# A planned order of work, by due time instead of merge order, and three small matmul groups of a head made one

## The chip, the cores and the metric

The kernel runs on one core of one Trainium2 chip. The metric is the device time of one execution in microseconds (us); the median of three runs of the kernel before is 2750.61 us (2749.08 to 2750.61). One execution was taken with the hardware profiler. Engines are named as the profile names them: PE (TensorE, matrix products), PEld (its weight loads), DVE (VectorE), ACT (ScalarE), POOL (GpSimd) and SP (SyncE, which here only issues DMA transfers). SBUF is the on-chip working memory, PSUM the eight banks into which PE writes its products. 0.2%, 5.5 us, is about what a measurement of this kernel can tell from no change.

## The reference

Four transformer layers in a row work on x of shape 4 x 512 x 512 with a context of 4 x 64 x 512, all in float32.

- Layer 0: twice a cross attention to the context (16 heads of width 128, with one learned extra key and value per head), each behind a layer norm, then a GELU MLP of width 2048.
- Layer 1: a small cross attention of width 512 without heads, added with a factor alpha.
- Layer 2: x is the latent; its queries attend to the context (under an integer mask) and to x itself, 16 heads of width 32; then an RMS norm and an MLP of width 2048.
- Layer 3: a cross attention to the context under a boolean mask, 16 heads of width 32, and an MLP of width 2048, both behind layer norms.

```python
# layer 0, one of its two cross attentions (cut)
qh = (q_in @ wq + bq).reshape(b, q_len, H, K)
kh = jnp.concatenate([(kv_in @ wk + bk).reshape(b, t, H, K), bias_k], axis=1)
vh = jnp.concatenate([(kv_in @ wv + bv).reshape(b, t, H, K), bias_v], axis=1)
weights = jax.nn.softmax(jnp.einsum('bqhk,bthk->bhqt', qh, kh) / scale, axis=-1)
return jnp.einsum('bhqt,bthk->bqhk', weights, vh).reshape(b, q_len, H * K) @ wo + bo
```

## The kernel before

The kernel is a recording and a planner. The layer functions do not issue instructions; each `with pe(us)`, `with dve(n)`, `with either(n)` and so on records one operation (`Op`) with the engines on which it may run, a duration for planning, and the buffers that it takes and reads. An operation on PE can hold several matmuls; these are issued together, and this text calls them a group. `Plan.merge` then lays the recorded operations of streams that may run beside each other (`pl.beside`, for example the keys, the values and the token norms of layer 0) into one list. How far each stream stands at which share of the others is set by the table `PACES`: thirteen regions, two or three streams each, seventeen numbers per stream. An operation's `pos` is its place in that list, in microseconds of PE work.

`Plan.attempt` walks through time with a heap per engine. When an engine is free it takes the first ready operation of its heap that finds room in PSUM and SBUF and does not run more than `AHEAD` us (loads `AHEAD_LOAD`) of `pos` ahead of the oldest unfinished one. The heaps are in the order of the merged list (`op.n`, line 417). An operation that may run on two engines goes to whichever takes it first; the sums in SBUF (`added`, line 1046, recorded at line 1048) run on DVE or POOL, copies out of PSUM (`move`, lines 575 and 576) on ACT or DVE. A bank of PSUM or a block of SBUF is given back in the moment in which its last reader ends (line 519), while an operation that reads a result becomes ready 0.06 us after its maker ended (0.2 us after PE), plus 0.1 us if it goes to PE. What `attempt` puts out is the order in which each engine gets its instructions; on the chip every engine works through its own queue in order, and waits where a semaphore says so.

Layer 0 does not multiply x with wq. For each head it takes the head's keys K (built at line 717 as the product of wk and the context), multiplies them with the transposed wq of that head (line 812: four matmuls of 130 columns in two groups, each with a PSUM bank of its own) and with bq (line 823: one matmul, a third group and bank). For the values it takes V of a head (line 717 again, with wv) and multiplies it with that head's rows of wo (line 877). Two heads share a bank, one in its lower and one in its upper 64 partitions; there is one group for each of the two batches of a pair. Line 891 multiplies the extra value with wo. The attention itself (lines 933, 1038, 1367 and the softmax between them) and the MLPs (line 1089) use Strassen-like products of seven instead of eight parts, and the sums at line 1048 make their operands and put their results together. In layer 2, line 1571 makes the scores of four heads in four banks, line 1582 takes their maxima, line 1594 the exponentials, and line 1628 transposes these.

Three small transfers are issued ahead of the plan: alpha by ACT's queue, and the masks mk_i and mk_b by POOL's queue. All others are operations of SP in the plan.

Of the kernel before, what the change touches and what calls it, by code (L numbers as in the profile page):

```python
# [209 lines left out]
class Op:  # L210
    __slots__ = ("n", "pos", "engines", "calls", "wait", "next", "takes", "uses", "table", "ready", "start", "on", "load", "port")


class Plan:
# [11 lines left out]
    def __init__(self, sbuf, ahead, ahead_load, reserve, full, patience, near, paces):  # L226
        self.reserve, self.full = reserve, full * BLOCK
        self.sbuf = Memory(BLOCK, sbuf)
        self.psum = Memory(1024, 4)
        self.ahead, self.ahead_load = ahead, ahead_load  # L230
        self.patience, self.near, self.paces = patience, near, paces
        self.ops, self.regions = [], []
        self.pos = 0.0
# [143 lines left out]

    def order(self):
# [21 lines left out]
    def attempt(self, narrow):  # L400
# [3 lines left out]
        dma_free = 0.0  # L404
# [7 lines left out]
        out = []  # L412
        busy = dict.fromkeys(heaps, 0.0)

        def arm(op):
            for e in op.engines:
                heapq.heappush(heaps[e], (op.n, op))
# [6 lines left out]
        while left:  # L424
            progress = True
            while progress:
# [8 lines left out]
                for e, heap in heaps.items():  # L435
# [5 lines left out]
                    while heap and len(skipped) < 60:  # L441
                        n, op = heapq.heappop(heap)
                        if begun[n]:
                            continue
                        skipped.append((n, op))
                        if op.ready > now + 1e-9:
                            continue
                        if op.pos > limit + (ahead_load if op.load else ahead):
                            break
# [19 lines left out]
                    if second is not None and (choice is None or choice.pos > second.pos + 6.0):  # L469
                        choice = second  # L470
                    for n, op in skipped:
                        if op is not choice:
                            heapq.heappush(heap, (n, op))
# [35 lines left out]
            while events and events[0][0] <= now + 1e-9:  # L509
                _, kind, n = heapq.heappop(events)  # L510
                if kind != 1:
# [4 lines left out]
                for b in op.uses:  # L516
                    b.left -= 1
                    if b.left == 0:
                        b.mem.give(b)
# [128 lines left out]
def stack(nc, const, sbuf, psum, a, out):  # L648
# [15 lines left out]
    alpha = const.tile([P, 1], FP, name="alpha")  # L664
    nc.scalar.dma_start(out=alpha, in_=a["alpha"].to_broadcast([P, 1]))

    mk_i = const.tile([P, B * T], I32, name="mk_i")
    nc.gpsimd.dma_start(out=mk_i, in_=a["mask_i"].to_broadcast([P, B * T]))
    mk_b = const.tile([P, B * T], U8, name="mk_b")
    nc.gpsimd.dma_start(out=mk_b, in_=a["mask_b"].to_broadcast([P, B * T]))  # L670
    pl = Plan(BLOCKS, AHEAD, AHEAD_LOAD, RESERVE, FULL, PATIENCE, NEAR, PACES)
    sb, ps = pl.sb, pl.ps
    ctxT = pl.held(const.tile([P, NC * B * T], FP, name="ctxT")).v(NC, B * T)
    mterm2, mterm3 = (pl.held(const.tile([P, B * T], FP, name=f"mterm{i}")).v(B, T) for i in (2, 3))

# [110 lines left out]
    def l0_keys(n, half, bp):  # L786
# [6 lines left out]
        for j in range(4):  # L793
            for e in range(2):
# [12 lines left out]
                made = []  # L807
                for r in range(2):
                    p = ps()
                    with pe(4 * SHORT) as o:  # L810
                        for c in range(2):
                            o.matmul(
                                p[:, c * KP : (c + 1) * KP],
                                wq[:, (2 * r + c) * P : (2 * r + c + 1) * P],
                                kT.v(),
                                start=True,
                                stop=True,
                            )
                    made.append(p[:, : 2 * KP].split(2, KP))

                p = ps()
                with pe(2 * SHORT) as o:
                    o.matmul(
                        p[:, :KP], col(f"L0_xattn_bq{n}", h).to_broadcast([P, P]), kT.v(), start=True, stop=True
                    )

# [26 lines left out]
    def l0_values(n, half, bp):  # L853
# [6 lines left out]
        for j in range(HH):  # L860
# [11 lines left out]
            if j % 2:  # L872
                for i in range(2):
                    p = ps()
                    with pe(PAIR + 0.04) as o:
                        for e in range(2):
                            o.matmul(
                                p[e * T : (e + 1) * T, :],
# [4 lines left out]
                            )  # L883
                    with either(D) as o:
                        o.move(U[i].v(HH // 2, D)[:, j // 2, :].k(j // 2), p.v())
# [601 lines left out]
    def l2_context():  # L1487
# [5 lines left out]
        with pool(256) as o:  # L1493
            o.tensor_tensor(apart[:, 256:].k(1), row[:, 256:], row[:, :256], ALU.subtract)
        with dve(256) as o:
            o.tensor_scalar(mterm2, mk_i.rearrange("p (b s) -> p b s", b=B), 0.0, -3.0e38, ALU.is_equal, ALU.mult)
# [192 lines left out]
    def l3_context():  # L1689
        row = load_row("L3_xattn_v_b")  # L1690
        with dve(256) as o:
            o.tensor_scalar(mterm3, mk_b.rearrange("p (b s) -> p b s", b=B), 0.0, LOWEST, ALU.is_equal, ALU.mult)
# [127 lines left out]
    def a0():  # L1820
        l1.append(l1_project())
        l2_context()
# [6 lines left out]
    def a3(pair):  # L1829
# [21 lines left out]
AHEAD, AHEAD_LOAD, RESERVE = 170.0, 90.0, 2  # L1851
FULL = 24


PATIENCE, NEAR = 7.0, 37.0
# [3 lines left out]
        [2, 7, 11, 22, 33, 23, 51, 60, 57, 66, 72, 60, 77, 83, 93, 101, 104],  # L1859
        [-4, 6, 18, 24, 27, 26, 37, 42, 48, 66, 62, 76, 74, 81, 86, 92, 97],  # L1860
        [-1, 1, 14, 14, 28, 38, 37, 50, 54, 53, 61, 74, 76, 83, 90, 96, 111],
    ],
    [
        [-1, 8, 26, 23, 26, 28, 35, 43, 60, 61, 72, 61, 72, 72, 77, 79, 88],
        [18, 28, 34, 25, 39, 34, 60, 34, 55, 62, 73, 70, 77, 98, 92, 102, 111],
    ],
    [
        [4, 13, 16, 19, 27, 36, 40, 46, 37, 58, 68, 63, 67, 76, 86, 86, 87],
# [103 lines left out]
```

## Time and profile before

| | us |
|---|---|
| median of three runs | 2750.61 |
| the profiled execution | 2748.76 |
| its span, first to last instruction | 2747.0 |
| PE busy | 2701.2 (98%) |
| DVE busy | 2044.7 (74%) |
| POOL busy | 1323.0 (48%) |
| ACT busy | 931.5 (34%) |
| SP's queue (q1): share of 16 DMA engines | 19.4% |

In the profile's rows, a line such as L1089 is a line of the kernel file, `out<-in` are the tensors written and read (`arena` is all of the planned SBUF, `banks` all of PSUM), `xN` a number of hardware records. A float32 matmul leaves two records, since the hardware makes it in two passes; a transpose leaves one. The idle time of an engine stands behind the second bar with what ended it. Matmuls are pipelined, so that the busy time of PE also covers short waits between them.

### The profile page before, as it was taken

What the parts mean: (1) busy time and instruction counts of PE and PEld (TensorE: products, weight loads), DVE (VectorE), ACT (ScalarE), POOL (GpSimd) and SP (SyncE); (2) the same over time, 40 slices, a digit from 0 to 9 for tenths busy, and PEclk for the clock granted to TensorE, in tenths of its full rate; (3) what the DMA queues carried; (4) which work ended last, traced back from release to release, by engine and by line L of the source; (5) the groups of instructions that cost most, each with busy time, mean ns of one, the idle gap of its engine ahead of it and who ended that gap; (6) DMA issues with size and microseconds to landing.
All of it is one profiled execution on the core that took longest, in us unless ns stands there. A gap on an engine that the chain in (4) does not pass through costs nothing. (4 is left out here: it accounts for less than half of the span.)

```text
span 2747.0 us, 34916 instructions
## 1 busy us (share of the span) xinstructions
PE 2701.2 (98%) x12012; PEld 1648.4 (60%) x12012; DVE 2044.7 (74%) x3661; ACT 931.5 (34%) x1759; POOL 1323.0 (48%) x1465
## 2 busy tenths in 40 slices
PE   8999999999999999999999999999999999999999
PEld 6877778788854455556555665555544545454444
DVE  6788778786864577776787678687877878878655
ACT  3223242142331114453463255154523223333211
POOL 5567576574842262333335232424745485646421
PEclk9999999999999999999999999999999999999999
DMA  7222423243121020010102011110211120202200
GB/s 242 84 89 81 131 77 115 64 134 93 50 62 57 16 69 20 20 59 14 44 25 88 8 31 45 56 32 24 70 50 35 41 67 20 58 8 84 77 16 31
DMA packets 230368, 164.06 MB, mean 60 GB/s; under 512 B 9088, under 2 KB 198656, under 8 KB 230192
## 3 DMA queue, kind: packets, MB, share of 16 engines
q1 hardware_dynamic: 229824, 161.52, 19.4%
q8 instruction: 96, 1.57, 0.2%
q14 instruction: 80, 0.66, 0.1%
q0 software_dynamic: 80, 0.16, 0.0%
q10 hardware_dynamic: 288, 0.15, 0.0%
HBM read 157.60 MB, written 4.19 MB: 59 GB/s over the span
## 5 line engine op out<-in xcount | busy, mean ns | idle before, releaser
L1048 POOL TENSOR_TENSOR arena<-arena 128x256 f32<-128x256 f32 (+4 forms) x1016 | 1064.1, 1064 | 970.5 <-DVE arena L576 169.8
L1089 PE MATMUL banks<-arena 128*128 128x512 f32 x2688 | 1201.9, 594 | 7.9 <-DVE arena L1108 2.6
L1089 PEld LDWEIGHTS banks<-arena 128*128 128x128 f32 x2688 | 497.8, 190 | 578.3 <-issue 497.6
L1048 DVE TENSOR_TENSOR arena<-arena 128x256 f32<-128x256 f32 (+4 forms) x664 | 574.1, 879 | 89.9 <-POOL arena L1048 24.8
L575 ACT COPY arena<-banks 128x512 f32<-128x512 f32 (+4 forms) x563 | 280.5, 516 | 793.9 <-PE banks L1089 196.3
L1367 PE MATMUL banks<-arena 128*128 128x256 f32 x1792 | 408.3, 380 | 3.2 <-DVE arena L938 1.5
L1367 PEld LDWEIGHTS banks<-arena 128*128 128x128 f32 x1792 | 336.2, 190 | 79.8 <-issue 21.9
L576 DVE COPY arena<-banks 128x512 f32<-128x512 f32 (+2 forms) x353 | 213.1, 613 | 160.2 <-PE banks L1089 52.5
L1124 ACT ACTIVATE arena<-arena,cols 128x512 f32<-128x512 f32 x192 | 138.0, 722 | 313.2 <-DVE arena L1048 172.9
L1108 DVE TENSOR_TENSOR arena<-banks,arena 128x512 f32<-128x512 f32 x240 | 163.8, 685 | 90.6 <-PE banks L1089 76.2
L933 PE MATMUL banks<-arena 128*128 128x260 f32 x896 | 212.0, 385 | 0.3 <-DVE arena L938 0.2
L1594 ACT ACTIVATE arena<-banks,arena 128x512 f32<-128x512 f32 x256 | 174.7, 687 | 95.1 <-DVE arena L1584 49.5
L933 PEld LDWEIGHTS banks<-arena 128*128 128x128 f32 x896 | 163.5, 188 | 36.0 <-ACT arena L575 3.0
L1582 DVE TENSOR_REDUCE arena<-banks 128x1 f32<-128x512 f32 x256 | 167.5, 681 | 13.3 <-PE banks L1571 12.2
L717 PE MATMUL banks<-ctxT,arena 128*128 128x128 f32 (+1 forms) x1152 | 164.1, 292 | 12.1 <-DMA arena<-in_L_wv 6.5
L717 PEld LDWEIGHTS banks<-ctxT,arena 128*128 128x128 f32 x1152 | 148.8, 194 | 29.5 <-issue 11.2
L1628 PEld LDWEIGHTS banks<-ident,arena 128*128 128x128 f32 x1024 | 116.5, 141 | 81.6 <-issue 35.1
L1628 PE MATMUL banks<-ident,arena 128*128 128x128 f32 x1024 | 140.9, 276 | 3.5 <-ACT arena L1594 2.9
L717 PE MATMUL banks<-arena 128*128 128x512 f32 (+2 forms) x432 | 140.4, 482 | 0.0
L1147 DVE TENSOR_TENSOR arena<-banks,arena 128x512 f32<-128x512 f32 x144 | 98.2, 685 | 50.2 <-PE banks L1089 50.1
L1605 POOL TENSOR_TENSOR arena<-arena 128x256 f32<-128x256 f32 x64 | 39.5, 617 | 188.6 <-DVE arena L1584 160.2
L717 PEld LDWEIGHTS banks<-arena 128*128 128x128 f32 x432 | 72.4, 191 | 68.3 <-issue 65.7
(155 smaller groups left out, 2528.4 us busy)
## 6 DMA issues: line engine op xcount, KB each, us to landing
arena<-in_L_w SPq DMA_DIRECT2D x192, 256.0 KB, 3.3
arena<-in_L_wk SPq DMA_DIRECT2D x80, 256.0 KB, 4.9
arena<-in_L_wv SPq DMA_DIRECT2D x64, 256.0 KB, 5.6
arena<-in_L_wqT SPq DMA_DIRECT2D x64, 256.0 KB, 5.5
arena<-in_L_wo SPq DMA_DIRECT2D x64, 256.0 KB, 5.7
arena<-in_L_wq SPq DMA_DIRECT2D x32, 256.0 KB, 3.3
arena<-in_L_wo SPq DMA_DIRECT2D x8, 1024.0 KB, 5.4
arena<-in_L_wv SPq DMA_DIRECT2D x6, 1024.0 KB, 5.7
```

Of the source, the lines that this page charges most:

```text
L575: "ACT": lambda e, out, in_: e.copy(out, in_),
L576: "DVE": lambda e, out, in_: e.tensor_copy(out, in_),
L717: o.matmul(dst, lhs(c), rhs(c), start=(c == 0), stop=(c == NC - 1))
L933: o.matmul(p[:, : 2 * KP], lhs(c), rhs(c, b % 2), start=(c == 0), stop=(c == 1))
L1048: o.tensor_tensor(out, x, y, op)
L1089: o.matmul(p.v(), lhs(c), rhs(c), start=(c == 0), stop=(c == 1))
L1108: o.tensor_tensor(t.v(), p.v(), y.v(), ALU.add)
L1124: o.activation(g[f].v(), src.v(), func, bias=col(b1, q * NC + f))
L1367: o.matmul(p[:, i * 256 : (i + 1) * 256], lhs(c), rhs(c), start=(c == 0), stop=(c == 1))
L1582: o.tensor_reduce(m[:, i : i + 1].k(i), banks[i].v(), AX.X, ALU.max)
L1594: o.activation(y.v(), banks[i].v(), AF.Exp, bias=nm[:, i : i + 1].k(i), scale=qs, accum_out=sums[:, i : i + 1].k(i),)
L1628: o.transpose(p[:, c * P : (c + 1) * P], e[i][:, c * P : (c + 1) * P], ident)
```

## The change

Five things are edited. The planner's heaps for work that touches neither PSUM nor PE are now sorted by due time: the earliest `pos` at which PE needs the result, less the durations on the way. Memory is given back later: 0.06 us after its last reader ended (0.2 us after PE), and 0.1 us more for a PSUM bank. An operation that is too far ahead is passed over, where the search stopped before. The products of a head's K with wq and bq become one group of five matmuls with three banks, and the products of V with wo for both batches one group of four matmuls with two banks. The transfers of alpha and of the two masks become operations of SP in the plan. The planner's numbers and the whole of `PACES` have new values.

```diff
+        due = [1e9] * len(merged)
+        for op in reversed(merged):
+            at = op.pos if "PE" in op.engines else 1e9
+            for o in op.next:
+                at = min(at, due[o.n])
+            if "PE" not in op.engines:
+                at -= min(op.engines.values()) + 0.1
+            due[op.n] = at
+            held = any(b.mem is self.psum for b in op.uses)
+            op.key = op.pos if held or op.load or "PE" in op.engines else min(at, op.pos + 200)
...
-        dma_free = 0.0
+        dma_free = 1.5
...
-                heapq.heappush(heaps[e], (op.n, op))
+                heapq.heappush(heaps[e], (op.key, op.n, op))
...
                         if op.pos > limit + (ahead_load if op.load else ahead):
-                            break
+                            continue
...
-                    if second is not None and (choice is None or choice.pos > second.pos + 6.0):
+                    if second is not None and (choice is None or choice.pos > second.pos + self.switch):
...
+                if kind == 2:
+                    freed[n].mem.give(freed[n])
...
                     if b.left == 0:
-                        b.mem.give(b)
+                        at = now + (self.AFTER_PE if op.on == "PE" else self.AFTER)
+                        if b.mem is self.psum:
+                            at += self.BEFORE_PE
+                        heapq.heappush(events, (at, 2, len(freed)))
+                        freed.append(b)
...
-    alpha = const.tile([P, 1], FP, name="alpha")
-    nc.scalar.dma_start(out=alpha, in_=a["alpha"].to_broadcast([P, 1]))
-    mk_i = const.tile([P, B * T], I32, name="mk_i")
-    nc.gpsimd.dma_start(out=mk_i, in_=a["mask_i"].to_broadcast([P, B * T]))
-    mk_b = const.tile([P, B * T], U8, name="mk_b")
-    nc.gpsimd.dma_start(out=mk_b, in_=a["mask_b"].to_broadcast([P, B * T]))
+    mk_i, mk_b = (pl.held(const.tile([P, B * T], t, name=f"mk{i}")) for i, t in ((2, I32), (3, U8)))
+    alpha = pl.held(const.tile([P, 1], FP, name="alpha")).v()
...
-                made = []
-                for r in range(2):
-                    p = ps()
-                    with pe(4 * SHORT) as o:
-                        for c in range(2):
-                            o.matmul(
-                                p[:, c * KP : (c + 1) * KP],
-                                wq[:, (2 * r + c) * P : (2 * r + c + 1) * P],
...
-                    made.append(p[:, : 2 * KP].split(2, KP))
-                p = ps()
-                with pe(2 * SHORT) as o:
+                banks = [ps() for _ in range(3)]
+                with pe(10 * SHORT) as o:
+                    for c in range(NC):
+                        o.matmul(
+                            banks[c // 2][:, c % 2 * KP : (c % 2 + 1) * KP],
+                            wq[:, c * P : (c + 1) * P],
...
                     o.matmul(
-                        p[:, :KP], col(f"L0_xattn_bq{n}", h).to_broadcast([P, P]), kT.v(), start=True, stop=True
+                        banks[2][:, :KP], col(f"L0_xattn_bq{n}", h).to_broadcast([P, P]), kT.v(), start=True, stop=True
                     )
+                made = [q[:, : 2 * KP].split(2, KP) for q in banks[:2]]
+                p = banks[2]
...
-                for i in range(2):
-                    p = ps()
-                    with pe(PAIR + 0.04) as o:
+                banks = [ps() for _ in range(2)]
+                with pe(2 * PAIR - 0.1) as o:
+                    for i in range(2):
                         for e in range(2):
                             o.matmul(
-                                p[e * T : (e + 1) * T, :],
+                                banks[i][e * T : (e + 1) * T, :],
...
+        load(mk_i.v(), a["mask_i"].to_broadcast([P, B * T]), 256)
...
+        load(mk_b.v(), a["mask_b"].to_broadcast([P, B * T]), 256)
...
+        load(alpha, a["alpha"].to_broadcast([P, 1]), 8)
...
-AHEAD, AHEAD_LOAD, RESERVE = 170.0, 90.0, 2
-FULL = 24
-PATIENCE, NEAR = 7.0, 37.0
+AHEAD, AHEAD_LOAD, RESERVE = 150.0, 112.0, 4
+FULL = 23
+PATIENCE, NEAR, SWITCH = 7.25, 35.0, 2.0
 PACES = [
     [
-        [2, 7, 11, 22, 33, 23, 51, 60, 57, 66, 72, 60, 77, 83, 93, 101, 104],
...
+        [40, 41, 48, 23, 14, 12, 31, 46, 52, 66, 70, 77, 79, 92, 89, 87, 100],
...
```

## The prediction

> **What bounds the kernel now.** I read the busy shares first, then TensorE's waits, then the timeline at three places.
>
> ```profile
> span 2747.0 us, 34916 instructions
> PE 2701.2 (98%) x12012; PEld 1648.4 (60%) x12012; DVE 2044.7 (74%) x3661; ACT 931.5 (34%) x1759; POOL 1323.0 (48%) x1465
> PEclk9999999999999999999999999999999999999999
> L1089 PE MATMUL banks<-arena 128*128 128x512 f32 x2688 | 1201.9, 594 | 7.9 <-DVE arena L1108 2.6 <-DVE arena L1048 1.5 <-DVE arena L1147 1.2
> ```
>
> PE is busy 98% of the span, so only what delays PE counts. But the 98% hides waits: one pass over 512 columns is shown with 594 ns, while passes that follow each other start every 429 ns. A wait of 100 ns between two passes therefore shows as no idle time. From the starts of the matmuls in the trace, the steady steps are 429 ns (512 columns), 222 (260), 216 (256), 112 (128 or 130) and 109 (transposes). Laid end to end at these steps, and at the usual step of the packed products, the 12,012 records take 2617 us; from the first start (6.5 us) to the last (2742.1) they take 2735.6. So 118.5 us are lost between PE's groups of matmuls (a group: what the kernel issues under one `with pe`), 6.5 before them and 4.9 after. That is all that a new order can win.
>
> ```profile
> PE banks L717 <- DMA arena<-in_L_wv: 6.5, 1, 6.5
> PE banks L717 <- DMA arena<-in_L_wk: 4.6, 1, 4.6
> PE banks L1571 <- ACT arena L1594: 4.5, 5, 1.7
> PE banks L1628 <- ACT arena L1594: 2.9, 5, 0.8
> PE banks L1089 <- DVE arena L1108: 2.6, 3, 1.2
> PE banks L1571 <- ACT arena L575: 2.1, 4, 0.7
> ```
>
> These are the visible waits (us in total, times, longest). The first two are the start. Of the rest, L1571 behind L1594 and L575, and L1089 behind L1108, wait for a PSUM bank to be emptied; L1628 behind L1594 waits for data. One of them in the timeline (start us, us; in brackets the idle time before):
>
> ```profile
> 1066.86 0.60 PE L1628 MATMUL banks<-ident,arena 128*128 128x128 f32 x4
> 1067.50 0.58 ACT L575 COPY arena<-banks 128x512 f32<-128x512 f32 x1 [0.57 <-PE banks L1628]
> 1068.14 1.14 PE L1571 MATMUL banks<-arena 32*128 32x512 f32 x8 [0.67 <-ACT arena L575]
> ```
>
> L1571 needs the bank that L1628 has just filled. L1628's last pass ends at 1067.46, the copy takes 0.58, and L1571 starts 0.06 after it.
>
> **The change, part by part.** No arithmetic is added or removed: 6,974 matmuls before and after. Built, both files give the order in which each engine gets its work, so its effect can be counted.
>
> *The order (due times, banks given back late, new paces).* For each PE group I take its place on PE with all groups before it laid end to end at the steps above, and the earliest time at which its banks are emptied and its operands made: end of the PE group that feeds the chain, 0.2 us, the chain's instructions at their median durations (ACT copy 0.58, DVE sum out of a bank 0.69, POOL sum 0.73 or 1.29), 0.06 between engines and 0.1 into PE (these three are the planner's own allowances). The difference is the group's margin; queues in front of those engines are left out. For the kernel before, the loss really measured on entering each group can be set beside it (margin: groups before, their loss in us, mean; groups after, loss at the same mean):
>
> - under -0.6: 18, 22.0, 1.222; 17, 20.8
> - -0.6 to -0.15: 34, 6.4, 0.188; 26, 4.9
> - -0.15 to 0: 102, 10.5, 0.103; 5, 0.5
> - 0 to 0.3: 178, 11.7, 0.066; 161, 10.6
> - 0.3 to 1: 782, 29.7, 0.038; 714, 27.1
> - over 1: 1240, 38.1, 0.031; 1271, 39.0
>
> Sum: 118.4 before, 102.9 after, **-15.5 us**. The one large entry is the third: 97 groups no longer enter a bank that is still being emptied. The old planner gave a bank back in the instant its last reader ended; the new one adds 0.16 to 0.3 us. The first entry hardly moves. Ends: 0, if the 97 groups lose elsewhere what they lost here, and -36, if the groups over 1 us, whose loss can only come from queues that the margin leaves out, lose half as much under the due times. I take -15.5, the value at the means that were measured.
>
> *The merged groups.* V wo (L877): 44 lone pairs took 1.01 us each from start to next start, 10 that stood two in a row 1.91 (lowest 1.87). After, all 32 stand two in a row: 63.6 us become 32 x 1.90 = 60.8, so -2.8; part of it is already in the margins' means, so -2.0 (ends 0 and -3.9). The wq and bq products keep their passes (10 of 112 ns a head); 128 of the 160 groups that vanish are theirs, and their loss is in the list. What the merge adds is a wait for three banks at once, with all later PE work queued behind it; only 5 groups of any line enter in the third class, so nothing beyond the list.
>
> *The start.* alpha, mk_i and mk_b leave the ACT and POOL queues; the loads are reordered (now value weights first).
>
> ```profile
> 6.50 2.05 PE L717 MATMUL banks<-ctxT,arena 128*128 128x128 f32 x8 [6.50 <-DMA arena<-in_L_wv]
> 13.19 2.05 PE L717 MATMUL banks<-ctxT,arena 128*128 128x128 f32 x8 [4.64 <-DMA arena<-in_L_wk]
> 216.44 1.16 PE L717 MATMUL banks<-ctxT,arena 128*128 128x128 f32 x8 [0.91 <-DVE arena L576]
> mk_i<-in_mask_i POOLq DMA_DIRECT2D x1, 128.0 KB, 6.5
> ```
>
> Landings: ctxT 4.47, alpha 6.21, first wv 6.37, mk_i 8.09, mk_b 9.10, rows 9.44, then a 256 KB load every 0.7 to 0.85 us, wk at 13.06. Without the three small ones I put wv at 5.3 and the tenth load, which the first V wo group needs (the second wo), at 11.7. The first passes run at half speed (2.05 us for x8 against 1.16 later, though the clock row shows full). After: lead 5.4, two wv products of 1.8 each to 9.0, idle to 11.75: 8.2 idle against 6.5 + 4.6 + 0.5 = 11.6. The slow stretch is about as long in both. -3.4, taken as **-3** (ends: +1, if the small loads delayed nothing and only the new order counts; -5).
>
> *What costs nothing.* The three loads now stand in SP's queue, 0.5 us of issue each, in stages where DMA is 10 to 20% busy; if that cover were gone, the mask term would be late by one landing, 6.5 us. Table loads on ACT go from 89 to 77, 12 x 1.28 = 15 us less, on an engine that is 34% busy. Sums of L1048 move from DVE (664 to 624) to POOL (1,016 to 1,056).
>
> [...]
>
> ```profile
> 351.20 2.35 POOL L1048 TENSOR_TENSOR arena<-arena 128x1024 f32<-128x1024 f32 x1
> 351.71 2.13 DVE L1048 TENSOR_TENSOR arena<-arena 128x260 f32<-128x260 f32 x1
> ```
>
> A DVE sum that takes 0.43 alone took 2.13 beside POOL's. All 664 take 574 us, 213 more than at their undisturbed durations: 0.21 us per POOL sum, so 40 more stretch DVE by 8 us. PE waited 1.5 us in all for L1048 on DVE, so I count 0. [...]
>
> **Sum.** -15.5 - 2 - 3 = -20.5. The profiled execution took 2748.8 (span 2747.0 and 1.8 around it), 1.8 below the median of the runs, 2750.6. From the median: **2730 us** (0.7% faster).
>
> **The rivals.**
> - *The due times also shorten the queues* (0.17): the groups over 1 us lose half, -19.5 more: 2711. For it: DVE at 74% was served in merge order, whoever's result was due first. Against it: operations due within 0.5 us of their PE reader rise from 524 to 563.
> - *Only groups and start pay* (0.15): the margins' gain turns up as other waits; -5: 2745.6. For it: the large losses (under -0.6) stay 17 groups.
> - *Slower: late data in layer 2's attention* (0.12). The groups with operands (not banks) later than -0.6 go from 2 to 11, nearly all transposes of exponentials (L1628 before) in two clusters. At 1.2 us that is +11, inside the list. If ACT's queue there makes as many again late three times over (+33), and the third class pays nothing (+10), the sum is +22: 2773. It decides once more than 17 further groups are late at 1.2 us.
>
> That the edit does not do what it says is excluded: the built order shows the groups merged.
>
> **How the numbers follow.** The likeliest case holds 0.56. Its own range is 2718 to 2742. The range 2706 to 2748 takes in the first rival but for its tail and the second, and leaves the slower one out with half of what exceeds it. 0.2% (5.5 us) is what a measurement here can tell from no change: faster is the first two and half of the third (0.80), same the other half and a margin (0.08), slower the rest (0.12).
>
> **What would show it.** Right: entries that lose about 0.1 us (between 0.06 and 0.15: 242 now, 123 of them before 780 us) clearly fewer before 780 us; first matmul at 5.3 to 5.7; V wo groups at 1.9. Wrong: the loss between 1000 and 2450 us, 61 of the 118 now, grows, with waits on L1594 or its successor ahead of the transposes; or a first V wo group that starts after 14 us.

## The result and the profile after

The changed kernel takes 2717.6 us (median of four runs, 2715.7 to 2720.8) against 2749.9 for the kernel before (four runs, 2749.1 to 2750.6). The ratio is 0.9884, with a 95% interval of 0.9867 to 0.9901: 32 us faster, where 20.5 were forecast. The profiled execution took 2720.8 (span 2719.0), the longest of the four. Against the profiled execution of before (2748.8) that is -28.0; the other 4 us lie between profiled executions and medians, 3.1 above after's and 1.1 below before's.

The page after: the span, the busy shares, the granted clock and the costliest matmul group.

```profile
span 2719.0 us, 35021 instructions
PE 2686.5 (99%) x12012; PEld 1651.1 (61%) x12012; DVE 2016.2 (74%) x3617; ACT 913.6 (34%) x1751; POOL 1361.5 (50%) x1503
PEclk9999999999999999999999999999999999999999
L1101 PE MATMUL banks<-arena 128*128 128x512 f32 x2688 | 1199.5, 595 | 5.1 <-DVE arena L1120 3.6
```

The lines have moved: L1101 is L1089 of before, L1641 (transposes of the exponentials) L1628, L1584 (scores of layer 2) L1571, L888 (V wo) L877, L825 and L832 (K with wq and bq) L812 and L823, L731 (keys and values) L717, L1379 L1367, L1060 L1048, L592 L575. The share of 99% again says little; TensorE's busy time fell by 14.7 us and the span by 28.0, with the same 12,012 records, so waits of both kinds went, the visible and those hidden within busy time.

TensorE's largest visible waits after, and that of the scores (us in total, times, longest):

```profile
PE banks L1641 <- ACT arena L1607: 8.4, 7, 3.8
PE banks L731 <- DMA arena<-in_L_wv: 6.3, 2, 5.2
PE banks L1101 <- DVE arena L1120: 3.6, 6, 1.8
PE banks L1584 <- ACT arena L592: 1.0, 3, 0.5
```

The wait for the key weights (4.6) is gone. The scores no longer wait for banks behind the exponentials (4.5 before). The transposes wait for their exponentials longer than before (2.9).

The loss between TensorE's groups, counted as the prediction counts it, went from 118.5 to 87.2 us, the lead from 6.5 to 5.2, the tail from 4.9 to 4.7. These fall by 32.8, not 28.0, since 4.8 is a change of the books: inside a merged V wo group the hand-over from one pair to the next is now part of its steady step (1.867 us from start to next start, against 2 x 0.858, which is four steps of 429 ns). Kept apart so that nothing is counted twice, the 28.0 come from three places:

| place | before | after | difference |
|---|---|---|---|
| start: lead, and loss before 40 us | 6.5 + 10.7 | 5.2 + 7.9 | -4.1 |
| V wo after 40 us: loss on entering it, and the next group behind it, with the 4.65 of the books (31 groups: all but the first, two of them ahead of 40 us) added back | 7.2 + 9.8 | 2.5 + 2.7 + 4.65 | -7.1 |
| all other groups after 40 us | 90.8 | 74.1 | -16.7 |

By stage, the loss before 780 us (layer 0) fell from 46.7 to 22.0, and between 1000 and 2450 us only from 61.0 to 56.7. The last row of that table, sorted by margin ("groups: loss in us"; V wo, the group behind it and the start left out):

| margin, us | before | after |
|---|---|---|
| under -0.6 | 16: 15.0 | 16: 16.5 |
| -0.6 to -0.15 | 28: 5.2 | 24: 7.3 |
| -0.15 to 0 | 83: 7.5 | 5: 0.3 |
| 0 to 0.3 | 132: 5.0 | 146: 6.3 |
| 0.3 to 1 | 747: 25.0 | 682: 12.7 |
| over 1 | 1204: 33.2 | 1235: 31.1 |

So 7.2 us left with the bank hand-overs that the prediction had counted, and 14.4 with groups that by their margins were never late (58.2 to 43.8; 29.8 ns a group before, 22.8 after). That second part is what the experiments had to explain. Its mean hides its shape: in a recount of the traces, the entries among these groups that lose over 0.3 us each went from 37 with 28.9 us to 23 with 13.6, and all the smaller ones together did not fall. So the gain there is some fourteen large losses fewer, not a little less at every group. The losses after also hold up to 6.8 us of passes at half clock, which the kernel before doesn't have (last section).

### The profile page after: what moved, and what is told of

The parts are those of the page before. It is cut to its first block, busy times and chain, and to the rows that moved or that the text cites. A ratio compares the mean times of both kernels' runs of the same rounds, so it can differ in the third digit from the quotient of the medians.

```text
span 2719.0 us, 35021 instructions
## 1 busy us (share of the span) xinstructions
PE 2686.5 (99%) x12012; PEld 1651.1 (61%) x12012; DVE 2016.2 (74%) x3617; ACT 913.6 (34%) x1751; POOL 1361.5 (50%) x1503
## 4 chain that ended last, share of the span: by engine, by line
PE 53%; DVE 4%; POOL 2%; issue 1%; ACT 1%; DMA 0%; POOLq 0%; SPq 0%; DVEq 0%; ACTq 0%
PE banks L1101 29%; PE banks L1379 6%; PE banks L731 5%; PE banks L1641 4%; PE banks L1584 2%; PE banks L1671 2%; POOL arena L1060 2%; DVE arena L1060 2%; PE banks L1432 1%; PE banks L1555 1%; PE banks L1661 1%; PE banks L1751 1%; PE banks L1742 1%; PE banks L1647 0%; DVE arena L1460 0%
## 5 line engine op out<-in xcount | busy, mean ns | idle before, releaser
L1060 POOL TENSOR_TENSOR arena<-arena 128x256 f32<-128x256 f32 (+4 forms) x1056 | 1107.7, 1068 | 925.0 <-DVE arena L593 131.4
L1101 PE MATMUL banks<-arena 128*128 128x512 f32 x2688 | 1199.5, 595 | 5.1 <-DVE arena L1120 3.6
L1101 PEld LDWEIGHTS banks<-arena 128*128 128x128 f32 x2688 | 497.9, 190 | 588.0 <-issue 519.4
L1060 DVE TENSOR_TENSOR arena<-arena 128x256 f32<-128x256 f32 (+4 forms) x624 | 543.9, 887 | 75.2 <-ACT arena L592 23.2
L592 ACT COPY arena<-banks 128x512 f32<-128x512 f32 (+3 forms) x571 | 283.6, 516 | 855.6 <-PE banks L1101 306.9
L1379 PE MATMUL banks<-arena 128*128 128x256 f32 x1792 | 403.4, 380 | 1.2 <-DVE arena L1060 0.5
L1379 PEld LDWEIGHTS banks<-arena 128*128 128x128 f32 x1792 | 337.5, 190 | 71.2 <-issue 20.9
L593 DVE COPY arena<-banks 128x512 f32<-128x512 f32 (+3 forms) x345 | 207.9, 613 | 139.9 <-PE banks L1101 42.0
L945 PEld LDWEIGHTS banks<-arena 128*128 128x128 f32 x896 | 164.8, 188 | 32.8 <-issue 4.5
L1641 PEld LDWEIGHTS banks<-ident,arena 128*128 128x128 f32 x1024 | 118.0, 143 | 79.2 <-issue 35.2
L731 PE MATMUL banks<-ctxT,arena 128*128 128x128 f32 (+1 forms) x1152 | 159.4, 290 | 6.3 <-DMA arena<-in_L_wv 6.3
L731 PEld LDWEIGHTS banks<-ctxT,arena 128*128 128x128 f32 x1152 | 146.5, 193 | 25.7 <-issue 10.2
L1641 PE MATMUL banks<-ident,arena 128*128 128x128 f32 x1024 | 140.0, 279 | 8.5 <-ACT arena L1607 8.4
L731 PE MATMUL banks<-arena 128*128 128x512 f32 (+2 forms) x432 | 140.8, 482 | 0.0
L731 PEld LDWEIGHTS banks<-arena 128*128 128x128 f32 x432 | 72.7, 191 | 69.1 <-issue 67.0
```

Source lines behind the costliest of these rows:

```text
L592: "ACT": lambda e, out, in_: e.copy(out, in_),
L593: "DVE": lambda e, out, in_: e.tensor_copy(out, in_),
L731: o.matmul(dst, lhs(c), rhs(c), start=(c == 0), stop=(c == NC - 1))
L945: o.matmul(p[:, : 2 * KP], lhs(c), rhs(c, b % 2), start=(c == 0), stop=(c == 1))
L1060: o.tensor_tensor(out, x, y, op)
L1101: o.matmul(p.v(), lhs(c), rhs(c), start=(c == 0), stop=(c == 1))
```

## The experiments

Each was timed in three rounds beside the kernel before, on the same chip. All of them run the planner anew, so even a small edit can move the order everywhere; how much that alone costs is measured last, and it turns out as large as most of the single effects.

### The merged groups taken apart again

`after_split` puts both merges back as they were, `after_split_q` only the one of K with wq and bq:

```diff
-                banks = [ps() for _ in range(3)]
-                with pe(10 * SHORT) as o:
+                for r in range(2):
+                    p = ps()
+                    with pe(4 * SHORT) as o:
...
+                p = ps()
+                with pe(2 * SHORT) as o:
...
-                banks = [ps() for _ in range(2)]
-                with pe(2 * PAIR - 0.1) as o:
-                    for i in range(2):
+                for i in range(2):
+                    p = ps()
+                    with pe(PAIR + 0.04) as o:
```

> The changed kernel with only the merged groups undone: the products of K with wq again in two groups and that with bq in a third, V wo in one group for each batch; planner and numbers as changed. By the count of margins (same list and means as in the prediction) 18, 34, 10, 192, 795 and 1305 groups lose 112.4 us against 103.0 for the changed kernel, and V wo pays up to 3.8 us more in single pairs: 9 to 13 us slower than the changed kernel's 2717.6, so 2727 to 2731. Rival A, that the two merges bring nearly all of the layer 0 gain (24.6 us between the two traces before 780 us): 2740 or more. Rival B, that the merges bring nothing and the new order all: 2718 to 2721.

> The changed kernel with only the products with wq and bq split again into three groups; V wo stays merged. Margins 17, 28, 7, 175, 755, 1340: list 108.1 against 103.0, 4 to 6 us slower than 2717.6: 2722 to 2724. If the wq merge carried the whole cost of splitting both (10 us): 2728. If V wo carried it: 2718 to 2720.

Measured: `after_split` 2727.8 (0.9918, 0.9903 to 0.9932), 10.2 above the changed kernel; `after_split_q` 2720.5 (0.9897, 0.9883 to 0.9912), 2.8 above. Between these two lie 7.4 us for V wo. By a recount of the two traces as in the table, about 5 us of that stand at V wo and the group behind it (14.9 against 5.1, and 4.65 of the books); the rest stands in other groups, where a new order alone can put it. The groups of `after_split` by line, K with wq and V wo (the number behind the last bar is the visible idle time):

```profile
L827 PE MATMUL banks<-arena 128*128 128x130 f32 x512 | 71.1, 278 | 0.0
L892 PE MATMUL banks<-arena 128*64 128x512 f32 x256 | 67.5, 615 | 1.6 <-DMA arena<-in_L_wo 1.6
```

and of the changed kernel:

```profile
L825 PE MATMUL banks<-arena 128*128 128x130 f32 x512 | 68.8, 277 | 0.0
L888 PE MATMUL banks<-arena 128*64 128x512 f32 x256 | 65.5, 619 | 1.0 <-DVE arena L755 1.0
```

A mean of 278 against 277 ns for one record shows nothing; the cost is in starts that come later without idle time. From start to next start the products with wq and bq take 75.5 apart and 73.1 merged (80.6 in the kernel before, so that most of their gain comes with the order). In the margins over 0.3 us, V wo and the start left out, the split kernels lose 44.6 and 44.4, at 22.3 and 22.0 ns a group: the merges are not what made these groups cheaper.

### Memory given back at once

```diff
                     if b.left == 0:
-                        at = now + (self.AFTER_PE if op.on == "PE" else self.AFTER)
-                        if b.mem is self.psum:
-                            at += self.BEFORE_PE
-                        heapq.heappush(events, (at, 2, len(freed)))
-                        freed.append(b)
+                        b.mem.give(b)
```

> The changed kernel, but its planner gives memory back in the moment its last reader ends, as before. The margin class from -0.15 to 0 grows from 5 to 66 groups, the others stay within a few (17, 22, 66, 168, 719, 1202). If such an entry costs the 0.10 us that it cost before, this is 4 to 6 us slower than 2717.6: 2722 to 2724. If the late give-back is without effect: 2717 to 2719. If it carries the larger part of the gain: 2730 or more.

Measured: 2733.2 (0.9937, 0.9922 to 0.9952), 15.6 above the changed kernel. The groups between -0.15 and 0 come back, 66 of them instead of 5, but at 0.08 us each they lose only 5.4. The rest is elsewhere: margins over 0.3 us lose 54.4 instead of 43.8, 29.3 ns a group, as in the kernel before, and the entries over 0.3 us among them are 37 again, as before, with 24.4 us. Its waits (L1578 is L1584 of the changed kernel, L1549 a product of 256 columns in the same layer, L1601 the exponentials):

```profile
PE banks L1095 <- DVE arena L1114: 3.2, 4, 1.2
PE banks L1549 <- ACT arena L1601: 3.0, 1, 3.0
PE banks L1578 <- ACT arena L1601: 2.3, 2, 1.8
```

The scores' wait for the exponentials, 4.5 in the kernel before and absent after, is back with 2.3 us. The rival that the late give-back carries more than its class was the nearer one in the total. Whether these waits come from the early give-back or from the new order, this run alone doesn't say: a random move of the planner's numbers costs as much (below).

### Merge order instead of due times

```diff
-            op.key = op.pos if held or op.load or "PE" in op.engines else min(at, op.pos + 200)
+            op.key = op.pos
```

> The changed kernel with the heaps sorted by place in the merged list again (due times off), all else as changed. By the margins (26, 33, 9, 141, 700, 1285) 11.3 us slower than the changed kernel: 2729. If the due times also shorten the queues in front of DVE and POOL, the groups with margins over 0.3 us lose more as well, some 10 us on top: 2739. If the due times do nothing but move work about: 2715 to 2722.

Measured: 2739.2 (0.9959, 0.9945 to 0.9974), 21.6 above the changed kernel. The rival's total came out, but not by its reason: it says that shorter queues make the groups with a large margin cheap, and these lose 46.9 here against 43.8 (24.5 ns a group). What grows is the class under -0.6: 26 groups and 31.2 us instead of 17 and 20.9. Its waits:

```profile
PE banks L1641 <- ACT arena L1607: 11.8, 12, 3.4
PE banks L731 <- DMA arena<-in_L_wv: 5.6, 1, 5.6
PE banks L1379 <- DVE arena L593: 3.9, 2, 2.9
PE banks L1379 <- DVE arena L1416: 3.2, 1, 3.2
PE banks L888 <- DMA arena<-in_L_wo: 2.7, 1, 2.7
```

Two single waits of about 3 us ahead of L1379 (0.5 at the most in the changed kernel) and 3.4 more ahead of the transposes are work that was served too late. So what comes back without the due times is a few large waits, not many small ones; here too a part may belong to the new order as such.

### The small transfers back in front

```diff
+    alpha = const.tile([P, 1], FP, name="alpha")
+    nc.scalar.dma_start(out=alpha, in_=a["alpha"].to_broadcast([P, 1]))
+    mk_i = const.tile([P, B * T], I32, name="mk_i")
+    nc.gpsimd.dma_start(out=mk_i, in_=a["mask_i"].to_broadcast([P, B * T]))
...
-        load(mk_i.v(), a["mask_i"].to_broadcast([P, B * T]), 256)
```

> The changed kernel with alpha and the two masks loaded ahead of the plan again, by ACT's and POOL's queues. Margins nearly as in the changed kernel (list 104.4 against 103.0). If the three small loads delay the first ones, the first matmul starts at 6.3 to 6.5 us instead of 5.24, and the time is 1 to 4 us longer than 2717.6: 2719 to 2722. If they delay nothing: first matmul at 5.2, 2717 to 2719.

Measured: 2719.2 (0.9883, 0.9867 to 0.9900), 1.5 above the changed kernel, within the scatter of the runs. The first matmul, at 6.00, came earlier than the 6.3 to 6.5 that were expected, but later than in the changed kernel. The timeline of `after_masks`, and then of the changed kernel (start us, us; in brackets the idle time before):

```profile
6.00 2.04 PE L736 MATMUL banks<-ctxT,arena 128*128 128x128 f32 x8 [6.00 <-DMA arena<-in_L_wv]
```

```profile
5.24 2.05 PE L731 MATMUL banks<-ctxT,arena 128*128 128x128 f32 x8 [5.24 <-DMA arena<-in_L_wv]
8.32 2.08 PE L731 MATMUL banks<-ctxT,arena 128*128 128x128 f32 x8 [1.03 <-DMA arena<-in_L_wv]
10.33 1.97 PE L888 MATMUL banks<-arena 128*64 128x512 f32 x2
13.27 3.46 PE L888 MATMUL banks<-arena 128*64 128x512 f32 x6 [0.97 <-DVE arena L755]
```

One pair of executions is not enough for a size: all fourteen kernels compared here load context and first value weights as their first two loads on SP's queue, and the first matmul starts at 5.24 to 5.60 in the seven without the small transfers in front, at 5.66 to 6.68 in the seven with them. The ranges don't meet, and the means lie 0.74 us apart. The rest of the difference to the kernel before (6.50) is scatter between executions, not the order of the loads, which is the same up to there.

### The parts put into the kernel before, one at a time

`before_giveback` and `before_merged` get the code that the two experiments above took out; `before_due` gets the keys and the search that goes on:

```diff
+            op.key = op.pos if held or op.load or "PE" in op.engines else min(at, op.pos + 200)
...
-                            break
+                            continue
```

> The kernel before with only the late give-back in its planner. Margins 26, 39, 8, 179, 783, 1319: the third class goes from 102 to 8 (-9.7 us), the two with large losses grow: the list says 122.0 against 118.4, so 3.6 us slower, 2754. Rival B, that the give-back is worth by itself what its undoing cost in the changed kernel (15.6 us): 2735.

> The kernel before with only the two merges of groups; planner and numbers as before. By the margins (30, 35, 59, 171, 695, 1204) the list loses 124.0 us against 118.4, because the old planner, replanning, leaves 30 groups with margins under -0.6 instead of 18; V wo gets 3.8 us cheaper: 2 us slower than 2750, so 2752 (2745 to 2757). Rival A, that the merges are worth by themselves what their undoing cost in the changed kernel (10 us): 2740.

> The kernel before with only the due times in its heaps (and the search going on past operations that are too far ahead). Margins 25, 40, 98, 203, 766, 1222: the list says 128.2 against 118.4, 10 us slower, 2760. Rival C, that due times shorten the queues whatever else is planned (their removal cost the changed kernel 21.6 us, of which the margins explain 11): 2740 or less.

Measured: give-back alone 2746.3 (0.9991, 0.9981 to 1.0000), merges alone 2759.2 (1.0034, 1.0022 to 1.0046), due times alone 2751.5 (1.0009, 1.0000 to 1.0018). None of them gains anything that can be told from no change, and the merges lose 10 us. Neither the list nor the rivals said this of the merges. The other two lie between what the list said (2754 and 2760) and what the rivals said (2735 and 2740). The classes do show each part at work: with late give-back 8 groups are left between -0.15 and 0 (102 before), at 1.1 us instead of 10.5; with the merges V wo after 40 us loses 2.7 instead of 7.2 on entering. But each kernel also gains groups under -0.6: 26, 30 and 25, where before has 18. One reading is that something that every edit does costs as much as the edit gains.

### Are the planner's numbers fitted to its code?

The suspicion: `PACES` and the other numbers suit the code that they stand beside, and any edit loses this fit. Two kernels exchange the numbers, and two keep the code and move about 160 of the 527 entries of `PACES` at random by 1 or 2.

```diff
-AHEAD, AHEAD_LOAD, RESERVE = 150.0, 112.0, 4
-FULL = 23
+AHEAD, AHEAD_LOAD, RESERVE = 170.0, 90.0, 2
+FULL = 24
...
-        [40, 41, 48, 23, 14, 12, 31, 46, 52, 66, 70, 77, 79, 92, 89, 87, 100],
+        [2, 7, 11, 22, 33, 23, 51, 60, 57, 66, 72, 60, 77, 83, 93, 101, 104],
```

That is `after_oldnumbers`; `before_newnumbers` is the reverse. And `after_jitter`, with `before_jitter` in the same manner:

```diff
-        [40, 41, 48, 23, 14, 12, 31, 46, 52, 66, 70, 77, 79, 92, 89, 87, 100],
+        [42, 41, 49, 23, 13, 12, 31, 45, 52, 66, 70, 77, 79, 92, 89, 87, 100],
```

> The changed kernel with the planner's numbers and PACES of the kernel before (6.0 us where the old code had it fixed). Margins 26, 35, 9, 148, 766, 1210: the list says 115.3 against 103.0, 12 us slower than 2717.6: 2730. Rival D, that the numbers carry the gain and the code little: 2745 or more. Rival E, that the code carries it and the numbers are luck: 2715 to 2722.

> The kernel before with the changed kernel's PACES and planner's numbers, code as before. Margins 19, 27, 112, 209, 749, 1238: list 120.1 against 118.4, so 2752 (2748 to 2756). Rival D, that the new numbers carry most of the gain by themselves: 2735 or less. Theory F in its strict form, numbers fitted to one planner are worth no more to another than a random move: 2758 or more.

> The changed kernel with 157 of the 527 entries of PACES moved by 1 or 2 (per cent of a stream) at random, nothing else. Theory F, that the numbers are fitted to the planner and any replanning pays: margins 28, 31, 7, 151, 722, 1255, list 14 us above the changed kernel (28 instead of 17 groups under -0.6): 2730 to 2734. Rival, that such a small move of the paces is harmless and the losses of the single edits came from the edits: 2715 to 2722.

> The kernel before with 164 of the 527 entries of PACES moved by 1 or 2 at random. Theory F: its numbers were fitted too; margins 25, 37, 90, 215, 773, 1214, list 9 us above the kernel before: 2756 to 2762. If so, the late give-back alone (2746.3) and the due times alone (2751.5) gained some 10 us each over a replanned kernel before. Rival: 2747 to 2753, and the single edits gained nothing.

| kernel | us | against before | groups under -0.6, their loss |
|---|---|---|---|
| after_oldnumbers | 2737.7 | 0.9956 (0.9941 to 0.9971) | 26: 22.1 |
| after_jitter | 2732.4 | 0.9941 (0.9926 to 0.9955) | 28: 26.6 |
| before_newnumbers | 2767.9 | 1.0067 (1.0052 to 1.0082) | 19: 24.2 |
| before_jitter | 2771.7 | 1.0082 (1.0065 to 1.0099) | 25: 23.2 |

A random move of 1 or 2 costs the changed kernel 14.8 us and the kernel before 22. The new numbers in the old code lose 18, the old ones in the new code 20. So the numbers are no gain by themselves; they are fitted to their code, both times. How they were found is not on record. The expectation for `after_jitter` held; `before_jitter` and `before_newnumbers` came out 10 and 12 us above the upper ends of theirs, which makes the second a case of the strict form of theory F, and `after_oldnumbers` lies between the list and rival D. In `before_newnumbers` the lost fit is visible as a few single waits:

```profile
PE banks L1628 <- ACT arena L1594: 6.3, 6, 2.9
PE banks L1089 <- DVE arena L1108: 4.3, 4, 2.8
PE banks L1542 <- ACT arena L1594: 3.6, 1, 3.6
PE banks L1367 <- DVE arena L1404: 3.2, 1, 3.2
```

With this the single parts can be read again. Against the kernel before with lost fit (2771.7) give-back alone is 25 us better, due times 20, merges 12; with fitted numbers on both sides all parts together are worth 32, and with lost fit on both sides 39 (the two moved tables) or 30 (the exchanged ones). The parts overlap: taken out one by one they cost 15.6, 21.6, 10.2 and 1.5, which is 49 in sum. How far one random move differs from the next was not measured by runs; these figures rest on one of each. Counted in built orders alone, none of 72 such moves of the changed table has as few groups under -0.6 as its 17 (18 to 42).

### What made the groups with a margin cheaper

The twelve kernels and the two compared, sorted by how they give memory back: loss per group at margins over 0.3 us, V wo and the start left out.

| give-back | ns a group |
|---|---|
| late: the changed kernel, after_split, after_split_q, after_masks, after_mergeorder | 22.8, 22.3, 22.0, 22.6, 24.5 |
| late, other numbers or the old code: after_oldnumbers, after_jitter, before_giveback | 26.3, 27.1, 26.5 |
| at once: the kernel before, after_instant, before_merged, before_due | 29.8, 29.3, 31.2, 26.3 |
| at once, other numbers: before_newnumbers, before_jitter | 33.7, 39.0 |

All eight plans with late give-back lie between 22.0 and 27.1, all six without between 26.3 and 39.0; `before_due` alone reaches into the other range. The numbers matter besides. So plans with late give-back lose less where the margins saw nothing to lower, but that the give-back does it is not shown. Put into the kernel before it lowers the loss from 29.8 to 26.5 ns a group, and the due times, which leave the give-back as it was, lower it to 26.3. The entries over 0.3 us say the same: 37 in the kernel before and 23 in the changed one; 37 in `after_instant`, but also 37 in `after_jitter`, where the give-back is late; 28 with late give-back alone, 33 with due times alone. Lost fit and early give-back leave the same mark. What would speak for the give-back is argued only: the margins leave out queues, so a bank that the list takes for free 0.3 us early can be freed late by a queue in front of ACT or DVE, and 0.16 to 0.3 us of delay planned at every hand-over is a cushion for that. Passing over an operation that is too far ahead was never taken out by itself.

## Why the prediction was right and where it was not

*What bounds the kernel, and direction:* right. All of the gain is loss between groups and the lead. 2717.6 lies inside the range and just under the likeliest case's own range (2718 to 2742); the forecast was 12.4 us too slow. That is the usual error of the list by margin: put to the twelve kernels of the experiments, its middle value missed eight by 7 to 16 us, in both directions, and four by less than 3. So the range held by its width of 42 us, and the centre says less than it seems. Of the 12.4, 7.5 are in the profiled executions (-28.0 against -20.5) and 4.9 in how the two profiled executions lie in their runs.

*The list by margin* (-15.5): the failed step is "loss at the same mean" for margins over 0.3 us. Counted by place, 6.1 of the list's 15.5 belong to V wo and the start, and 9.4 to all other groups, where 16.7 were measured. There the third class did as said (-8.0 forecast, -7.2 measured), margins over 0.3 gave 14.4 instead of 1.5, and the three remaining classes took back 4.9 where the list had them unchanged; the passes at half clock, up to 6.8 us, lie mostly in these and could make that up alone. A mean that is measured under one planner is not a property of the group: it fell by a quarter under the new plan. The lower end of that term (-36; its own numbers give -35) had this in view, with the due times as the reason. The runs don't bear that reason out: without due times these groups stay cheap (24.5 ns). What made them cheaper, the late give-back or numbers that fit, stays open.

*The merged groups* (-2.0, ends 0 and -3.9) *and the start* (-3): with the 6.1 that the list held for them, 11.1 forecast and 4.1 + 7.1 = 11.2 measured. A V wo group takes 1.87 us from start to next start, as the lowest of the pairs did (1.90 was used); 32 of them are 59.7 us where 60.8 were forecast, so -3.9, the far end of that term. The first matmul came at 5.24 (5.3 forecast). The first V wo group did start before 11.75, at 10.33, but only with its first two passes; the rest waited to 13.27. The trace names L755 on DVE, a token statistic that V wo does not read. The second wo landed at 13.13, where 11.7 was forecast, 0.14 ahead of the matmul, and in `after_split_q` and `after_masks` the same wait ends 0.13 and 0.14 behind that landing, so it is a wait for the second wo. The slow stretch was not as long in both: the first record of a full clock begins at 19.84 before, 13.3 us behind the first matmul, and at 16.41 after, 11.2 us behind it; the steps between passes of 128 columns go from 214 to 111 ns there. "Nothing beyond the list" for the wait for three banks: TensorE shows no visible wait ahead of L825 or L832.

*The sums that moved to POOL*, counted as 0: POOL now runs 1,056 of the sums at L1060 and DVE 624, as forecast, DVE's busy time is 28 us shorter, and TensorE waits 0.8 us for L1060 on DVE (1.5 before) and 1.5 on POOL. The 8 us by which the sums on DVE were to be stretched did not show: all 624 take 214 us more than at the medians of those of their shape with no POOL instruction beside them, and by the same count the 664 of before took 219 more. No gain went missing there.

*The rivals.* That the due times also shorten the queues (2711): the size came halfway, by another cause; without due times the groups with a margin are nearly as cheap. That only groups and start pay (2745.6): out, since the large losses did stay at 17 groups, as its argument said, but what left the other classes did not turn up as new waits. The slower one, late data in layer 2's attention: the mechanism is there. Loss ahead of the transposes went from 9.4 to 15.4 us, ahead of the products that read them (L1661, L1648 before) from 3.5 to 8.0, and the stage from 1700 to 2000 us lost 18.9 instead of 15.7. But 10.2 us of that stage ran at half clock (last section), so up to 5.1 of its loss are slow passes and not late data, 2.9 of them in the products; with these taken off its loss would not have grown. In the same attention the scores lost 10.5 instead of 20.9. It is far from the 17 further groups that would decide.

*The signs.* Entries that lose 0.06 to 0.15 us ahead of 780 us became fewer: a recount of the two traces, which finds 114 where the prediction has 123, finds 73 after. The loss between 1000 and 2450 us did not grow, though the waits ahead of the transposes did.

## What to carry to other kernels

Where a planner has free numbers that were searched, an edit of its code has to be compared with the numbers fitted again, or with both sides' fit lost: here one random move of 1 or 2 in a table cost 15 us and another 22, as much as any part of the change gains. A planner that gives a resource back in the instant of its last use plans hand-overs on which the chip lost here: 102 groups entered a bank that was still being emptied, at about 0.1 us each, and late give-back left 10 such groups at most in every plan that had it. Whether it also helps where the slack looks ample is open. And when merged groups are accounted, the step inside the merged group has to be measured before it is compared, or a gain is counted twice.

## What the runs showed of the hardware

The granted clock falls to one half in the middle of a kernel whose TensorE is 99% busy. In the changed kernel's profile it does so for 3.41 us at 1371.5 and at 1856.2, and for 6.83 us at 1869.8; in the kernel before, between its start and its end, not at all. The row of the clock in forty slices doesn't show it, being full throughout. The busy times around the first of them (us of the stretch, then TensorE, its weight loads, DVE, ACT and POOL with their instructions, and the granted clock, the share of DMA and GB/s):

```profile
1367.00:1372.00 5.00, 1.20 (x11) 0.80 (x8) 5.00 (x10) 4.38 (x8) 3.65 (x3) 0.95 0.00 0
1372.00:1375.00 3.00, 3.00 (x16) 1.92 (x16) 1.72 (x7) 2.39 (x8) 2.18 (x4) 0.51 0.00 0
1375.00:1380.00 5.00, 4.48 (x53) 2.57 (x50) 4.29 (x12) 3.51 (x10) 0.29 (x1) 1.00 0.02 3
```

TensorE works 1.2 of the 5 us ahead of it, and then at 0.51. The timeline says why it stood:

```profile
1366.09 1.14 PE L1584 MATMUL banks<-arena 32*128 32x512 f32 x8
1366.20 1.28 ACT L1136 ACT_TABLE_LOAD   x1
1367.49 0.72 ACT L1136 ACTIVATE arena<-arena,cols 128x512 f32<-128x512 f32 x1
1368.35 5.05 POOL L1060 TENSOR_TENSOR arena<-arena 128x512 f32<-128x512 f32 x4 [5.11 <-ACT arena L1136]
1368.39 0.72 ACT L1136 ACTIVATE arena<-arena,cols 128x512 f32<-128x512 f32 x1
1368.67 0.96 DVE L1597 SCALAR_TENSOR_TENSOR arena<-arena 128x1 f32<-128x1 f32 x1
1369.71 1.28 ACT L1607 ACT_TABLE_LOAD   x1 [0.60 <-DVE arena L1597]
1371.01 0.69 ACT L1607 ACTIVATE arena<-banks,arena 128x512 f32<-128x512 f32 x1
1371.84 1.97 PE L1641 MATMUL banks<-ident,arena 128*128 128x128 f32 x8 [3.80 <-ACT arena L1607]
1373.74 1.70 PE L1584 MATMUL banks<-arena 32*128 32x512 f32 x8
```

ACT changes its table for two GELUs of the MLP and back for the next exponential, at 1.28 us each. The exponential needs a scaled maximum from DVE, whose one-column instruction at L1597 takes 0.96 us beside POOL's sums (0.15 in the median of all 256). So TensorE stands 3.8 us, from 1368.04 to 1371.84, and what comes next runs at the half clock: the eight records of L1584 take 1.70 us, those before the wait 1.14. The low stretches in this trace last once and twice 3.41 us at one half (0.51 in the second window above). Ahead of the first of them lie 3.41 us without a matmul, ahead of the other two not. The 3.41 us ahead of each of the three (columns as above):

```profile
1368.09:1371.50 3.41, 0.00 (x0) 0.00 (x0) 3.41 (x7) 2.80 (x5) 3.15 (x3) 1.00 0.00 0
1852.78:1856.19 3.41, 2.17 (x15) 1.09 (x11) 3.30 (x10) 2.53 (x7) 0.61 (x1) 1.00 0.00 0
1866.44:1869.85 3.41, 1.72 (x12) 0.84 (x8) 3.41 (x6) 3.25 (x9) 3.41 (x5) 1.00 0.58 208
```

Ahead of the second and the third TensorE was busy for 2.17 and 1.72 us, and its longest waits there were 0.95 and 1.36. So two of the three falls came behind nothing longer than a wait of 1.4 us. In the fourteen profiles the clock falls 32 times between 30 and 2700 us, each time a whole number of 3.413 us behind the profile's first record of a full clock. Cut into such windows, the one ahead of a fall holds between 0.8 and 3.4 us without a matmul. All 21 windows at full clock with 2.0 us or more were followed by a fall; of those with 0.8 to 1.9 us, 11 were and 106 were not. What else decides there is not shown.

In these stretches the transposes of L1641 start every 213 ns, elsewhere every 109. So half of 13.65 us, 6.8 us, is an estimate of the most that this costs in that execution. Over 66 runs of the thirteen kernels (the changed one and the twelve), each compared with the mean of its own kernel, the span rises by 1.8 us for each 0.001 that the mean granted clock falls (correlation -0.87; 0.001 of the span is 2.7 us). The changed kernel's spans are 2713.9, 2715.5 and 2716.2 at 0.999, and 2719.0 at 0.997 in the profiled execution. That fits the 3.1 by which the profiled execution lay above its median. Within a trace the price shows directly, as 1.70 us for records that take 1.14 otherwise; between runs, whether the lower clock costs the time, or both follow from longer waits, is not told apart.
